# Layer 1 experts: inputs loaded in quarters and turned by VectorE, late tiles in two runs, six of eight output groups combined beside the last tiles

## The chip, the cores and the metric

One core of one Trainium2 chip runs the whole program. The metric is device time in microseconds (us), the median of three runs. A profiled execution is a further run with its own time; all rows of the profile belong to that one. Engines are named as in the profile: PE is TensorE (PEld its weight loads), DVE is VectorE, ACT is ScalarE, POOL is GpSimd, SP is SyncE, which here only issues loads.

## The reference, cut to what matters

The program is a two-layer network on four images of 1024 tokens with 256 channels. Layer 0 (attention, then a mixture of experts) and the first half of layer 1 (selective scans in four directions) are not touched but for one copy. The change is in the second half of layer 1, a mixture of eight experts of which each token uses its best two:

```
logits = xt @ Wr + br
top_p, top_idx = top_k(softmax(logits), 2);  weights = top_p / sum(top_p)
xn = (xt - mean) * rsqrt(var + 1e-5)
for the two experts e of each token:
    xe = xn * ln_g[e] + ln_b[e]                      # 256
    h  = gelu(xe @ W1[e] + b1[e])                    # 1024
    y_e = h @ W2[e] + b2[e]                          # 256
x = x + sum over the two of weights[e] * y_e
```

## The kernel before, in words

**Slots.** Every (token, expert) pair gets a row, a slot, in a table `slots_x` in HBM (258 floats: 256 channels of the normalised token, the number of its result row, its best expert). An expert owns a region of the table; within it pairs stand in order of the images. `norm` (L1680) normalises an image: TensorE makes means (L1689), turns the tokens (L1701) and makes router products (L1703); ScalarE copies the turned tokens to `tok` (L1705), squares them (L1709), copies the products (L1710) and later scales `tok` by a factor that GpSimd raises to a power (L1714 to L1725). `route` (L1597) finds both experts of each token and its slots, on VectorE mostly. `scatter` (L1977) writes the rows, 16 indirect transfers per image, issued by GpSimd (L1981). For images 0 to 2 these are generators whose steps are taken between the operations of the scans (the class from L2005 on, whose order is written out by hand in `turn`, L2134). There the products of the routing lie in the spare of two PSUM buffers that the scans use in turn: TensorE may clear it for the next scan (L2052) only when ScalarE has read the routing out of it, and VectorE's backward scan (L2070) waits for the clearing. For image 3 the routing runs in the expert stage.

**Tiles.** A tile is 256 slots of one expert. `Tiles.fill` (L1574) turns the numbers of slots of each expert into two lists: 17 early tiles (`EARLY`), which images 0 to 2 fill for certain, and late tiles. 36 tiles (`USUAL`) are run; three more stand under a branch that is taken when `extra` says so (L2324). Per tile (class `Tile`, L2219):

- `slots` (L2231): one load of 128 x 2 x 258 floats. `weights` (L2236 to L2246): six loads, of which w1 and w2 are 1 MB each. All are issued by SP, which first reads the expert's or the block's number into a register. The weights have two buffers.
- `inputs` (L2250): TensorE transposes the tile in four 128x128 blocks into PSUM (L2254), VectorE scales it (L2257) and makes the list of result rows `to` (L2260).
- `hidden` (L2263): 16 products of 128x128 by 128x256 (32 matmul rows in the profile; L2269), with a gelu on ScalarE after each pair (L2271); three PSUM buffers of two pieces each.
- `result` (L2273): 16 more products (L2277, again 32 rows), the bias on VectorE (L2280), and two indirect transfers by GpSimd (L2282) that write each result row to its token's place in `results` in HBM. Unused slots go to spare rows at the end of `results`. The framework sees writes to one tensor and makes each wait for the one before.

In this stage the framework's scheduler orders the instructions. It takes two tiles' transposes together, ahead of the first one's matmuls.

**Combination** (L2326 on). When all tiles are done, eight groups of 512 tokens each load both results of each token (1 MB, L2336, by SP), ScalarE multiplies the first by its weight (L2343), VectorE adds the weighted second (L2344), TensorE transposes back (L2347, eight rows), VectorE adds to `x` (L2350), and GpSimd issues two stores (L2351).

Of the kernel before, what the change touches and what calls it, by code (L numbers as in the profile page):

```python
# [11 lines left out]
F32 = mybir.dt.float32  # L12
# [9 lines left out]
P = 128  # L22
# [17 lines left out]
T = 256  # L40
NTILE = 2 * B * L // T + E - 1
# [6 lines left out]
FIRST, SECOND = (2 * (i + 1) * L // T + E - 1 for i in range(2))  # L48
# [14 lines left out]
def metaformer(ctx: ExitStack, tc: tile.TileContext, t: dict, out: bass.AP):  # L63
# [81 lines left out]
    results = dram.tile([2 * B * L + 2 * P, C], F32, tag="results", name="results")  # L145
# [1417 lines left out]
    class Tiles:  # L1563
# [8 lines left out]
        def fill(self, room, tiles, begun):  # L1572

            ends, leap = room([E]), room([E])  # L1574
            past, use, block = room([self.size, E]), room([self.size, E]), room([self.size])
            nc.vector.tensor_tensor_scan(ends, one[:, :E], tiles, 0.0, ALU.mult, ALU.add)
            nc.vector.tensor_tensor(past, ids[:, : self.size].unsqueeze(2).to_broadcast([P, self.size, E]),
                                    ends.unsqueeze(1).to_broadcast([P, self.size, E]), ALU.is_ge)
            nc.vector.tensor_reduce(self.expert, past, AX.X, ALU.add)
            nc.vector.tensor_scalar(self.expert, self.expert, float(E - 1), None, ALU.min)  # L1580

            nc.vector.tensor_tensor(leap, begun[:, 1:], begun[:, :E], ALU.subtract)
            nc.vector.tensor_tensor(leap, leap, tiles, ALU.subtract)
            nc.vector.tensor_scalar(leap, leap, float(BLOCKS), None, ALU.add)
            nc.vector.tensor_tensor(use, past, leap.unsqueeze(1).to_broadcast([P, self.size, E]), ALU.mult)
# [10 lines left out]
    def route(b, tok, slot, space, psum, tag):  # L1596
# [49 lines left out]
        nc.vector.tensor_tensor(place, place, region.unsqueeze(2).to_broadcast([P, E, NT]), ALU.add)  # L1646
        nc.vector.tensor_tensor(count, count, cum[:, :, NT - 1], ALU.add)
# [11 lines left out]
        counts = count.unsqueeze(2).to_broadcast([P, E, BLOCKS])  # L1659
        limits = marks.unsqueeze(1).to_broadcast([P, E, BLOCKS])  # L1660
        if b == B - 2:

            nc.vector.tensor_tensor(more, counts, limits, ALU.is_ge)
            nc.vector.tensor_reduce(tiles, more, AX.X, ALU.add)
            ends = early.fill(room, tiles, done)
            nc.vector.tensor_tensor(left, tiles, ends, ALU.subtract)
            nc.vector.tensor_scalar(left, left, float(EARLY), 0.0, ALU.add, ALU.max)
            nc.vector.tensor_tensor(done[:, :E], left, tiles, ALU.min)
            yield
            yield  # L1670
        else:

            nc.vector.tensor_scalar(count, count, float(T - 1), None, ALU.add)
            nc.vector.tensor_tensor(more, counts, limits, ALU.is_ge)
            nc.vector.tensor_reduce(tiles, more, AX.X, ALU.add)
            nc.vector.tensor_tensor(tiles, tiles, done[:, :E], ALU.subtract)
            ends = late.fill(room, tiles, done)
            nc.vector.tensor_scalar(extra, ends[0:1, E - 1 : E], USUAL - EARLY + 0.5, None, ALU.is_gt)

    def norm(b, tok, pool, psum, tag, raw_tag, d):  # L1680
# [14 lines left out]
        for r in range(NT // 2):  # L1695
# [9 lines left out]
            nc.scalar.copy(tok[:, ts(r, 2), :C], tp)  # L1705
# [270 lines left out]

    def scatter(b):  # L1977

        for n in range(NT):
            for k in range(2):  # L1980
                nc.gpsimd.indirect_dma_start(  # L1981
                    out=slots_x, out_offset=bass.IndirectOffsetOnAxis(ap=slot[:, k, n : n + 1], axis=0),
                    in_=tok[:, n], in_offset=None)
                yield
# [229 lines left out]
    with ExitStack() as st:  # L2214
        of_tiles = st.enter_context(ExitStack())
        pb = of_tiles.enter_context(tc.tile_pool(name="m1_b", bufs=2))
        blocks = slots_x.rearrange("(k a p) c -> k p a c", a=T // P, p=P)

        class Tile:  # L2219
            def __init__(self, tiles, i, tag="xs", bufs=4):  # L2220
                self.tiles, self.i = tiles, i
                self.xs = pb.tile([P, T // P, W], F32, tag=tag, name=tag, bufs=bufs)
# [6 lines left out]
            def slots(self):  # L2229
                block = self.register(1, E * BLOCKS)  # L2230
                nc.sync.dma_start(self.xs, blocks[bass.ds(block, 1)].rearrange("o p a c -> p (o a) c"))  # L2231
# [16 lines left out]
            def inputs(self, ps_t):  # L2248


                tp = ps_t.tile([P, CT, T], F32, tag="tp", name="tp")
                for a in range(T // P):
                    for c in range(CT):
                        nc.tensor.transpose(tp[:, c, ts(a, P)], self.xs[:, a, ts(c, P)], ident)  # L2254
                self.xe = pb.tile([P, CT, T], F32, tag="xe", name="xe")
                for c in range(CT):
                    nc.vector.tensor_scalar(self.xe[:, c], tp[:, c], self.lng[:, c : c + 1],  # L2257
                                            self.lnb[:, c : c + 1], ALU.mult, ALU.add)
                self.to = pb.tile([P, T // P], I32, tag="to", name="to", bufs=NTILE)
                nc.vector.scalar_tensor_tensor(self.to, self.xs[:, :, C + 1], self.tiles.expert[:, self.i : self.i + 1],  # L2260
                                               self.xs[:, :, C], ALU.not_equal, ALU.add)
# [11 lines left out]
            def result(self, ps_y):  # L2273
# [7 lines left out]
                for a in range(T // P):  # L2281
                    nc.gpsimd.indirect_dma_start(  # L2282
                        out=results, out_offset=bass.IndirectOffsetOnAxis(ap=self.to[:, a : a + 1], axis=0),
                        in_=ys[:, a], in_offset=None)

        with ExitStack() as sa:
            pa = sa.enter_context(tc.tile_pool(name="m1_a", bufs=1))
            psa = sa.enter_context(tc.tile_pool(name="m1_psa", bufs=1, space=PSUM))
            ps_t = sa.enter_context(tc.tile_pool(name="m1_ps_t", bufs=2, space=PSUM))
            ps_h = sa.enter_context(tc.tile_pool(name="m1_ps_h", bufs=3, space=PSUM))  # L2290
            ps_y = sa.enter_context(tc.tile_pool(name="m1_ps_y", bufs=1, space=PSUM))

            def run(one_tile):
                one_tile.inputs(ps_t)
# [3 lines left out]
            todo = [Tile(early, i, "xa", EARLY) for i in range(EARLY)]  # L2298
            for i in range(EARLY):
                todo[i].slots()  # L2300
                if i < 2:
                    todo[i].weights()
            b = B - 1
            routing = chain(norm(b, tok, pa, psa, "t", "raw", pa.tile([P, CT, L], F32, tag="nm_d", name="nm_d")),
                            route(b, tok, slot, pa.tile([P, NUMBERS], F32, tag="numbers", name="numbers"), psa, "t"), scatter(b))
            for i in range(EARLY):
                run(todo[i])
                if i + 2 < EARLY:
                    todo[i + 2].weights()
                for _ in range(6):  # L2310
                    next(routing, None)
            assert next(routing, "end") == "end"

            def run_late(which):
                for i in which:
                    one_tile = Tile(late, i)
                    one_tile.slots()
                    one_tile.weights()
# [104 lines left out]
```

## Time and profile before

| | |
|---|---|
| three runs | 3966.72, 3970.53, 3973.8 us (median 3970.53) |
| profiled execution, time | 3952.81 us |
| its span, first to last instruction | 3951.0 us |
| mean clock granted to TensorE | 0.876 |
| busy: PE, DVE, ACT, POOL | 3373.9, 3017.3, 2789.5, 1936.6 us |
| last matmul of the scans' output `y` ends | 3361.8 us |
| first and last expert matmul of layer 1 (start, end) | 3371.0, 3902.9 us |
| loads of w1 and w2 of a tile | 1024 KB each, 5.4 and 5.5 us to landing |
| loads of a tile's inputs (L2231, late tiles) | 258 KB, 4.1 us to landing |

The page of the profile lists busy shares, a picture of the span in 40 slices, the DMA queues, the chain of work that ended last, the costliest groups of instructions and the loads. In a row of a timeline the first number is the start in us, the second the duration, then engine, line, operation, output <- input, shape and count; in brackets is how long the engine had been idle before and what ended that. In a row of the table by windows, the pairs are busy us and instructions (x) of PE, PEld, DVE, ACT and POOL, then the granted clock of TensorE, the DMA engines' share, and GB/s. All rows hold for one profiled execution.

### The profile page before, as it was taken

Reading aid. Unit: us, or ns where it says so; the run is one execution under the profiler, and the core shown is the slowest. Engines: PE = TensorE matmul, PEld = TensorE weight load, DVE = VectorE, ACT = ScalarE, POOL = GpSimd, SP = SyncE. Lnnn points to the kernel's source line nnn. Section 1 sums busy time; section 2 is a strip of 40 time slices with the busy share of each in tenths; the row PEclk is TensorE's granted clock in tenths of the full one; section 3 lists DMA queues with packets and bytes.
Section 4 is the critical chain, followed back from the end, with each engine's and each line's share of the span. In section 5 each row is a group of like instructions: output and inputs, shape, how many; then the busy total and the mean of one; then the engine's idle time right before and its main releaser. Section 6 shows DMA issues by size and latency. Waiting matters only on the chain. (4 is left out here: it accounts for less than half of the span.)

```text
span 3951.0 us, 49637 instructions
## 1 busy us (share of the span) xinstructions
PE 3373.9 (85%) x17330; PEld 1889.9 (48%) x17330; DVE 3017.3 (76%) x5164; ACT 2789.5 (71%) x3738; POOL 1936.6 (49%) x1675
## 2 busy tenths in 40 slices
PE   8378888888788888886697889998998989999996
PEld 5134444534353444543475333443443433788885
DVE  3689899989989898999476899999999999211112
ACT  2889999899989999996244677777767766322222
POOL 0145544675648475575343766556555556121111
PEclk9567887788778777788798999999999999999997
DMA  9400084000000000000384434334334334755555
GB/s 283 121 1 1 1 230 128 1 1 31 12 1 1 1 33 1 1 12 17 97 243 133 142 119 139 118 107 127 120 112 127 125 112 128 223 183 185 189 192 188
DMA packets 241814, 393.71 MB, mean 100 GB/s; under 512 B 31888, under 2 KB 182160, under 8 KB 241424
## 3 DMA queue, kind: packets, MB, share of 16 engines
q1 hardware_dynamic: 218016, 340.54, 28.4%
q0 software_dynamic: 19904, 48.48, 3.8%
q8 instruction: 139, 2.28, 0.2%
q10 hardware_dynamic: 3632, 1.40, 0.1%
q14 instruction: 123, 1.01, 0.1%
HBM read 280.41 MB, written 109.94 MB: 99 GB/s over the span
## 5 line engine op out<-in xcount | busy, mean ns | idle before, releaser
L825 POOL TENSOR_SCALAR dr<-s_n,last 128x1024 bf16<-128x1024 f32 x250 | 715.6, 2880 | 729.5 <-DVE state L853 421.5
L735 ACT ACTIVATE junk_a<-s_n,state 128x1024 int8<-128x1024 f32 x448 | 514.7, 1149 | 23.6 <-DVE state L859 7.3
L2081 POOL TENSOR_TENSOR da_c<-prod,come 128x1024 f32<-128x1024 f32 x128 | 257.5, 2012 | 378.8 <-DVE h L2087 322.7
L739 DVE TENSOR_SCALAR_CACHE_REDUCE junk_v<-s_n,state 128x1024 int8<-128x1024 f32 x320 | 408.6, 1277 | 8.8
L2271 ACT ACTIVATE hid<-hp,b 128x256 f32<-128x256 f32 x288 | 134.1, 474 | 361.1 <-PE hp L2269 361.1
L786 DVE SCALAR_TENSOR_TENSOR w<-s_n,win 128x1024 f32<-128x1024 f32 x256 | 352.0, 1375 | 5.3
L789 DVE MAX8 win<-w 128x8 f32<-128x1024 f32 x256 | 314.5, 1228 | 8.8
L2070 DVE TENSOR_TENSOR_SCAN sum<-da,uu 128x1024 f32<-128x1024 f32 x127 | 289.7, 2281 | 26.5 <-PE sum L2052 19.1
L2092 PE MATMUL sum<-h,ident 128*128 128x512 f32 x512 | 261.4, 635 | 55.6 <-DVE h L2087 52.4
L893 ACT ACTIVATE ex<-sT 128x1024 f32<-128x1024 f32 x256 | 246.9, 1016 | 82.9 <-PE sT L885 82.6
L2046 POOL TENSOR_TENSOR uu<-dx,bb 128x1024 f32<-128x1024 f32 x127 | 303.6, 2390 | 1.7 <-DMA bb<-bc_d 1.6
L735 ACT ACTIVATE junk_a<-s_n,guess 128x1024 int8<-128x1024 f32 x256 | 294.2, 1149 | 7.2
L2063 DVE TENSOR_TENSOR_SCAN h<-da,uu 128x1024 f32<-128x1024 f32 x127 | 288.1, 2269 | 1.0 <-POOL uu L2046 1.0
L2087 DVE TENSOR_TENSOR_SCAN h<-da_c,uu 128x1024 f32<-128x1024 f32 x127 | 288.5, 2272 | 0.0
L2058 PE MATMUL sum<-da_c,ident 128*128 128x512 f32 x512 | 257.2, 626 | 27.3 <-POOL da_c L2081 23.8
L903 PE MATMUL o_ps<-ex,vT 128*32 128x256 f32 x2048 | 236.2, 450 | 50.1 <-ACT ex L893 35.7
L2280 DVE TENSOR_TENSOR ys<-yp,b2e 128x512 f32<-128x512 f32 x36 | 24.9, 691 | 325.7 <-PE yp L2277 325.7
L2030 ACT ACTIVATE da_c<-delta,a_log 128x1024 f32<-128x1024 f32 x128 | 268.0, 2094 | 5.2 <-DMA rows_y<-ys 5.1
L2269 PE MATMUL hp<-xe,w 128*128 128x256 f32 x1152 | 259.0, 383 | 9.4 <-DVE xe L2257 5.9
L2282 POOL DMA_INDIRECT results<-ys,to x72 | 69.3, 963 | 397.0 <-DVE ys L2280 183.6
L769 ACT COPY s_n<-sp 128x1024 f32<-128x1024 f32 x256 | 245.5, 1003 | 23.7 <-PE sp L761 16.0
L2277 PE MATMUL yp<-w2e,hid 128*128 128x256 f32 x1152 | 255.6, 380 | 0.0
(675 smaller groups left out, 7513.9 us busy)
## 6 DMA issues: line engine op xcount, KB each, us to landing
cb<-bc_d SPq DMA_DIRECT2D x128, 512.0 KB, 4.1
bb<-bc_d SPq DMA_DIRECT2D x127, 512.0 KB, 5.0
w<-in_w SPq DMA_DIRECT2D x36, 1024.0 KB, 5.4
w2e<-in_w SPq DMA_DIRECT2D x36, 1024.0 KB, 5.5
slots_x<-zeros SPq DMA_DIRECT2D x1, 33669.0 KB
slots_x<-zeros SPq DMA_DIRECT2D x1, 33282.0 KB
w<-in_w SPq DMA_DIRECT2D x72, 256.0 KB, 3.2
xs<-slots_x SPq DMA_DIRECT2D x36, 261.0 KB, 3.4
```

Of the source, the lines that this page charges most:

```text
L735: nc.scalar.activation(junk, self.row(r), AF.Sign, bias=thr, scale=-1.0, accum_out=u)
L739: nc.vector.tensor_scalar(junk, self.row(r), thr, None, ALU.is_lt, ALU.add, accum_out=u)
L786: nc.vector.scalar_tensor_tensor(w, self.row(r), self.win[:, r, 0:1], self.row(r), ALU.is_gt if r < LAST_DVE else ALU.is_ge, ALU.subtract, ...
L789: nc.vector.max(out=self.win[:, r, 1:], in_=w)
L825: ins = eng.tensor_scalar(dr, self.row(r), self.last[:, r : r + 1], None, ALU.is_lt)
L2030: nc.scalar.activation(grid(self.da_c), cols_flipped(self.prep.delta[:, self.c]), AF.Exp, scale=self.decay)
L2046: nc.gpsimd.tensor_tensor(self.uu[:, 0], self.prep.dx[:, self.c], self.bb, ALU.mult)
L2063: nc.vector.tensor_tensor_scan(rows.rearrange("p r w -> p (r w)"), self.da, self.uu[:, 0], 0.0, ALU.mult, ALU.add)
L2070: nc.vector.tensor_tensor_scan(self.sum[:, ::-1], self.da[:, ::-1], self.uu[:, 0][:, ::-1], 0.0, ALU.mult, ALU.add)
L2087: nc.vector.tensor_tensor_scan(self.hs, self.da_c, self.uu[:, 1], 0.0, ALU.mult, ALU.add)
L2092: nc.tensor.matmul(cols_flipped(self.sum[:, ts(h, HALF)]), ident, grid(self.hs)[:, :, ts(h, half)], start=False, stop=False)
L2269: nc.tensor.matmul(hp[:, f % 2], self.w1[:, c, ts(f, P)], self.xe[:, c], start=(c == 0), stop=(c == CT - 1))
```

## The change

1. **Source order** (`quarters`): when ScalarE copies turned tokens to `tok`, it permutes the channels from (c, q, i) to (q, c, i), with c of 2 halves, q of 4 quarters and i of 32. One copy becomes two.
2. **Quarters**: a tile's inputs are loaded by four loads, one per quarter of the partitions, of 32 x 8 pieces of 64 floats, and a fifth for the two marks of each slot. Tiles are loaded four ahead (`AHEAD`). VectorE transposes 128x512 at once, each 32x32 block by itself, which with the order above gives channels by tokens; then it scales from there. TensorE's transposes and their PSUM buffers go.
3. **Result rows**: `to` is made of three VectorE operations; unused slots get spare rows of their own for each tile, so that no two transfers write the same row, and the framework is told so (`rows_of_their_own`): these writes no longer wait for one another. The same is said of the scatters.
4. **Late tiles in two runs**: first, per expert, all tiles with slots of images 0 to 2; then the rest. After tile 30 (`THIRD` - 1) all results of images 0 to 2 exist.
5. **A written order**: the stage stands in a hand-written order (`usual`): hidden of tile n, inputs of tile n + 1, steps of routing or combination, result of tile n, weights of tile n + 2, slots of tile n + 4, more steps. The 16 scatters of image 3 are issued at once, ahead of tile 13's result.
6. **Combination beside the tiles**: after tile 30 GpSimd issues the loads of the six groups of images 0 to 2; from tile 32 on (`n > THIRD`, 31) each of the two gaps of a tile takes a step: add and store one group, transpose the next, weight the one after; the eight steps end with tile 35. Image 3's two groups come at the end, each loaded in four pieces by SP and ScalarE.

The diff, cut to its core:

```diff
+S = 32
+AHEAD = 4
-FIRST, SECOND = (2 * (i + 1) * L // T + E - 1 for i in range(2))
+FIRST, SECOND, THIRD = (2 * (i + 1) * L // T + E - 1 for i in range(3))
...
         else:
-            nc.vector.tensor_scalar(count, count, float(T - 1), None, ALU.add)
-            nc.vector.tensor_tensor(more, counts, limits, ALU.is_ge)
-            nc.vector.tensor_reduce(tiles, more, AX.X, ALU.add)
-            nc.vector.tensor_tensor(tiles, tiles, done[:, :E], ALU.subtract)
-            ends = late.fill(room, tiles, done)
+            both_, begun = room([2 * E]), room([2 * E + 1])
+            nc.vector.tensor_copy(begun[:, :E], done[:, :E])
+            nc.vector.memset(begun[:, 2 * E :], 0.0)
+            nc.vector.tensor_scalar(tiles, before, float(T - 1), None, ALU.add)
+            whole_tiles(begun[:, E : 2 * E], tiles)
+            nc.vector.tensor_tensor(both_[:, :E], begun[:, E : 2 * E], done[:, :E], ALU.subtract)
+            yield
+            nc.vector.tensor_scalar(tiles, count, float(T - 1), None, ALU.add)
+            whole_tiles(left, tiles)
+            nc.vector.tensor_tensor(both_[:, E:], left, begun[:, E : 2 * E], ALU.subtract)
+            yield
+            ends = late.fill(room, both_, begun, 2 * E)
...
-            nc.scalar.copy(tok[:, ts(r, 2), :C], tp)
+            for c in range(CT):
+                nc.scalar.copy(quarters(tok[:, ts(r, 2), :C])[:, :, c],
+                               tp[:, :, ts(c, P)].rearrange("p n (q i) -> p n q i", i=S))
...
+    def rows_of_their_own(ins, group):
+        tc.declare_no_dep(ins, group=group, reason="rows of their own")
+        tc.add_to_no_dep_group(group, ins)
...
-                nc.sync.dma_start(self.xs, blocks[bass.ds(block, 1)].rearrange("o p a c -> p (o a) c"))
+                self.xs = pb.tile([P, T // S, width], F32, tag="xs", name="xs", bufs=AHEAD + 1)
+                for q in range(P // S):
+                    nc.sync.dma_start(self.xs[ts(q, S)], pieces[q][bass.ds(block, 1)].rearrange("o t i c -> t (o i) c"))
+                self.meta = pb.tile([P, T // P, W - C], F32, tag="meta", name="meta", bufs=AHEAD + 1)
+                nc.sync.dma_start(self.meta, marked[bass.ds(block, 1)].rearrange("o p a c -> p (o a) c"))
...
-                tp = ps_t.tile([P, CT, T], F32, tag="tp", name="tp")
-                for a in range(T // P):
-                    for c in range(CT):
-                        nc.tensor.transpose(tp[:, c, ts(a, P)], self.xs[:, a, ts(c, P)], ident)
+                xt = pb.tile([P, T // S, CT, S], F32, tag="xt", name="xt")
+                nc.vector.transpose(xt.rearrange("p i c t -> p (i c t)"), self.xs.rearrange("p i c -> p (i c)"))
...
+            def load(self):
+                self.y = pc.tile([P, 4, 2 * C], F32, tag="y", name="y")
+                if self.b < B - 1:
+                    ins = nc.gpsimd.dma_start(self.y, by_pairs[self.g]).ins
+                    rows_of_their_own(ins, "last_results")
+                    nc.gpsimd.memset(apart, 0.0)
+                else:
+                    for i in range(4):
+                        (nc.scalar if i % 2 else nc.sync).dma_start(self.y[:, i], by_pairs[self.g][:, i])
...
+        def combining():
+            for g in range(len(some) + 2):
+                if g > 1:
+                    some[g - 2].store()
+                if 0 < g <= len(some):
+                    some[g - 1].turn()
+                if g < len(some):
+                    some[g].combine()
+                yield
...
+            def between(n):
+                for _ in range(2):
+                    next(routing, None)
+                if n > THIRD:
+                    next(combined, None)
+
+            todo[0].inputs()
+            for n in range(USUAL):
+                todo[n].hidden(ps_h)
+                if n + 1 < USUAL:
+                    todo[n + 1].inputs()
+                between(n)
+                if n == EARLY - AHEAD:
+                    assert next(routing, "end") == "end"
+                    for _ in scatter(b):
+                        nc.gpsimd.memset(apart, 0.0)
+                todo[n].result(ps_y)
+                if n == THIRD - 1:
+                    for group in some:
+                        group.load()
+                if n + 2 < USUAL:
+                    todo[n + 2].weights()
+                if n + AHEAD < USUAL:
+                    todo[n + AHEAD].slots()
+                between(n)
...
+        for group in groups[len(some) :]:
+            group.load()
+        for group in groups[len(some) :]:
+            group.combine()
+            group.turn()
+            group.store()
```

`turn` makes eight transposes of 128x128 into two PSUM buffers; `store` adds them to `x` and issues two stores; `combine` is ScalarE's product and VectorE's sum, four of each.

## The prediction

> **What bounds the kernel now.** I read the cores view first (one core, span 3951.0 us, mean clock 0.876), then the table by windows over the stretch that the change rewrites. Columns: busy time of each engine, clock granted to TensorE, share of the DMA engines, GB/s.
>
> ```profile
> 3350.00:3400.00 50.00, 47.05 (x209) 34.33 (x208) 15.38 (x37) 13.15 (x36) 4.83 (x4) 1.00 0.76 243
> 3800.00:3850.00 50.00, 49.28 (x235) 42.32 (x234) 7.05 (x15) 12.58 (x27) 6.73 (x7) 1.00 0.58 192
> 3900.00:3951.00 51.00, 18.47 (x78) 13.24 (x76) 23.73 (x49) 13.65 (x32) 10.65 (x18) 0.55 0.67 253
> ```
>
> In the expert stage TensorE is busy 49.3 of 50 us; VectorE has 7, the DMA engines 0.58. The last 51 us are another stage: TensorE is nearly idle there. TensorE's own timeline shows the period of a pair of tiles:
>
> ```profile
> 3786.07 1.04 PE L2254 MATMUL tp<-ident,xs 128*128 128x128 f32 x8
> 3787.47 7.19 PE L2269 MATMUL hp<-xe,w 128*128 128x256 f32 x32 [0.36 <-DVE xe L2257]
> 3794.50 7.07 PE L2277 MATMUL yp<-w2e,hid 128*128 128x256 f32 x32
> 3801.41 7.09 PE L2269 MATMUL hp<-xe,w 128*128 128x256 f32 x32
> 3808.33 7.07 PE L2277 MATMUL yp<-w2e,hid 128*128 128x256 f32 x32
> 3815.24 1.04 PE L2254 MATMUL tp<-ident,xs 128*128 128x128 f32 x8
> ```
>
> A pair takes 29.16 us (3787.47 to 3816.63), of which the four blocks of matmuls take 27.66 and the turning of the inputs, with the 0.36 us wait behind it, 1.50. Then the end of the whole timeline:
>
> ```profile
> 3902.93 0.69 DVE L2280 TENSOR_TENSOR ys<-yp,b2e 128x512 f32<-128x512 f32 x1 [13.14 <-PE yp L2277]
> 3906.56 0.96 POOL L2282 DMA_INDIRECT results<-ys,to  x1 [1.71 <-DMA results<-ys,to]
> 3915.93 1.71 ACT L2343 ACTIVATE y<-y,wts 128x256 f32<-128x256 f32 x4 [19.44 <-DMA y<-results]
> 3943.61 1.29 DVE L2350 TENSOR_TENSOR x<-op,x 128x512 f32<-128x512 f32 x2 [0.68 <-PE op L2347]
> ```
>
> From TensorE's last expert matmul, T = 3902.9, it is 13 us to the first product of the combination, then eight groups at 3.55 us each, then 6.1 us from the last addition's end (3944.9) to the end of the span: 48.1 us. So the program's end is 3371.0 (first expert matmul) + 531.9 + 48.1.
>
> **The change part by part**, against the profiled execution (span 3951.0, time 3952.81; the median of the three runs is 3970.53, 17.7 above it; I carry the difference over unchanged).
>
> (a) *TensorE no longer turns inputs.* 18 pairs at 1.50: **-27.0 us**, all on the path. VectorE takes it: one transpose of 128x512 and two scalings per tile. No row shows its transpose. The nearest row is the 128x512 addition, 0.69 us; the Trainium skill (VectorE: DVE Perf Modes, The three transpose paths) gives 311 ns for a 128x128 block in bf16, an estimate of 1.24 us for four. That page also advises TensorE for a 128x128 transpose when PSUM will do as destination. By that rule the change picks the wrong engine; by the windows row TensorE is the bound and VectorE has 43 of 50 us free. A tile asks VectorE for at most 1.24 + 1.07 (scalings) + 0.69 + three small operations of 0.2 = 3.6 us in 13.83, and the built order puts a tile's inputs one whole tile ahead. I take 0 on the path; only the first tile pays it. Gaining is excluded too.
>
> (b) *Inputs come in quarters.* A tile's 256 packets of 1032 B become 1024 of 256 B and 256 of 8 B. The hardware queue's row from 3500 to 3850 us (50218 packets, 58.38 MB, 52.3% of sixteen engines) gives 58 ns a packet. Today's transfers take 0.58 x 14.58 = 8.5 us of each tile. At no cost per packet but bytes, nothing changes; at 58 ns for each of 1280 packets, 4.7 us come and 0.9 go: 12.3 of 13.83 us, still under the period. The Trainium skill (DMA: Bandwidth & Descriptors, Specifications) sets 512 B as the least for full rate; charging 256 B as 512 B is an estimate of +0.26 MB, about 1 us at the 304 GB/s that the whole queue's row gives while busy. All three fit; 0 on the path, since inputs are asked for four tiles ahead.
>
> (c) *Start of the stage.* Before, tile 0's inputs are the first load; the first expert matmul waited for the last small weight, landed at 3370.2. Now w1, four small ones and w2 go first, then the quarters; in the built program the fourth quarter must await the completion of the load eight places earlier, the scale, which lands about 3369.2. It then lands behind w2 and three quarters, at about 3373.3; transpose and scaling 1.5 us: first matmul at about 3375, **+4** (+2 to +8). Between 3362 and 3371 TensorE did 6.5 us of image 3's routing: eight rows at 0.43, 22 raw at 0.12, four transposes at 0.11. The written-out order puts all of it after tile 0: **+6.5**. And TensorE now idles 12 us. The cost of idling is in these rows:
>
> ```profile
> 3404.00:3408.00 4.00, 2.49 (x12) 1.81 (x10) 1.76 (x9) 0.41 (x1) 3.58 (x6) 1.00 0.82 282
> 3408.00:3412.00 4.00, 2.05 (x6) 1.55 (x7) 1.50 (x8) 2.98 (x8) 2.01 (x3) 0.82 0.09 33
> 3412.00:3416.00 4.00, 4.00 (x15) 3.41 (x15) 0.00 (x0) 3.29 (x7) 0.00 (x0) 0.75 0.02 4
> ```
>
> After a 3.46 us stall the clock is 0.82 and 0.75 for 8 us, some 1.7 us lost: **+1.7** here.
>
> (d) *Routing in a written order.* That 3.46 us stall was ScalarE's eight scalings of the tokens waiting for GpSimd's powers. In the new order GpSimd reaches the second power only after tile 3's two scatters: end of tile 3's matmuls + 0.9 + 2.2 (two issues) + 2.9 (the chain 3406.08 to 3409.0) = 6.0; the scalings take 3.6; tile 4's activations stand behind them, from 9.7. TensorE fills three PSUM buffers (5.2 us) and waits until 10.6: 5.4 + 1.7 of clock = 7.1 against today's 5.2, **+1.9**.
>
> (e) *The early scatters lose their waits on one another* (157 us of GpSimd waiting on its own results): off the path, 0, except in the tail.
>
> (f) *Six of eight groups are combined beside tiles 32 to 35.* Their 48 transposes run at full clock, 1.04 us per eight (in the tail, at 0.50, 1.94): **+6.2** on TensorE. The 6 MB of loads are issued by GpSimd when all results of tiles 0 to 30 have landed: end of tile 30 + 0.9 + 1.1 + 5.3 = 7.3. For the software queue's pace, its page row (19904 packets of 2436 B in 3.8% of 16 x 3951 us) gives 121 ns a packet, 3.2 us per MB alone, 6.5 if it shares evenly with the weights. With issue and landing I take 9.5 us for the first group: there at 16.8. It is first asked for by ScalarE behind tile 32's activations, at 20.7, and by TensorE ahead of tile 33, at 27.7. The second, at 20 to 23.3, is asked for right behind the first; who waits for it are tile 33's activations, which three PSUM buffers let come as late as 32.9. **0** for the wait (0 to 8).
>
> (g) *The tail has two groups.* Scatters issue together: at T + 1.0 and 2.05, landed and seen 2.96 later: T + 5.0 instead of 6.6. Eight quarter-MB loads from two queues; the page's 256 KB loads take 3.2 us, and 2 MB at the tail's 401 GB/s 5.2: all there at about T + 12.2. Last product and sum 1.0, transposes 0.5, additions 1.3: T + 15. Then 6.1 as before, and 0.4 for the branch: T + 21.5. **-26.6** (-21 to -29).
>
> (h) *Tokens written in source order.* One copy of 128x512 becomes two of half size, 0.59 against twice 0.38, in 12 turns of the scans. There ScalarE's small row is followed by TensorE's clearing of a sum and by VectorE, which waits 0.68 us in each of these turns:
>
> ```profile
> 2530.62 0.59 ACT L1705 COPY tok<-sum 128x512 f32<-128x512 f32 x1 [0.89 <-PE sum L1703]
> 2531.99 0.16 ACT L1710 COPY lg<-sum 128x16 f32<-128x16 f32 x1
> 2532.24 0.60 PE L2052 MATMUL sum<-nought 128*128 128x512 bf16 x2
> 2532.93 2.30 DVE L2070 TENSOR_TENSOR_SCAN sum<-da,uu 128x1024 f32<-128x1024 f32 x1 [0.68 <-issue]
> ```
>
> 12 x 0.18 = **+2.2** (0 to 4).
>
> (i) *Two runs of late tiles* leave 36 tiles; the longer tables are some 20 more VectorE operations of 0.2 to 0.4 us under tile matmuls: 0. The 16 scatters of image 3 hold SP's queue (loads of tile 16's weights stand behind tile 17's inputs) until about 24 us after tile 12; those weights are due at 41: 0, or up to 5 if each scatter waits out its landing.
>
> Sum: -27.0 + 4 + 6.5 + 1.7 + 1.9 + 6.2 - 26.6 + 2.2 = **-31.1 us**. Span about 3920, profiled time 3922, median **3939**.
>
> **The rivals.**
> 1. *As summed*, 3930 to 3949: 0.53. A measurement of this kernel can tell about 0.2%, 8 us, from no change.
> 2. *More is hidden*: the first tile is ready like today's, no cold clock, ScalarE's wait in (d) as short as today's: -31.1 - 4 - 1.7 - 1.9, about 3931 or below. For it: the first loads meet emptier DMA engines than today (1.0 share from 3376 to 3400, when seventeen tiles' inputs are fetched at once). Against: the written order, which nothing can fill. 0.12.
> 3. *The loads of (f) and the weights slow each other*: TensorE waits once per tile in the last four for weights or a group, 4 us each: -15, 3955. For it: the 1.0 share wherever many loads meet. 0.17 (0.155 faster, 0.015 same).
> 4. *Slower: the software queue can't keep pace.* ScalarE takes the sixth group before tile 35's activations, wanted by about 65 after tile 30 (four tiles of 13.83, five turnings, 5.2 of buffers). The groups arrive at 16.8 + 5p; beyond p = 9.6 us per MB each further us costs five, beyond 15.8 (66 GB/s) the gain is gone. At 18: +11, 3981. Against: 3.2 to 6.5. 0.11.
> 5. *It doesn't do what it says*: small packets cost more than the mean packet, the DMA engines become the bound and the tile period stays near 14.5: a loss of 0.7 x 36 = 25 of the 31: -6, 3965. For it: the upper end of (b) is a share of 0.89. 0.07 (0.065 same, 0.005 faster).
>
> Faster 0.53 + 0.12 + 0.155 + 0.005 = 0.81, same 0.08, slower 0.11. The range 3928 to 3959 takes in cases 1 and 2 and most of 3, and leaves 4 and 5 out.
>
> **What would show it.** Right: no input transposes on TensorE, tile period 13.8, first expert matmul near 3377 (scans 2 us longer), one 5 us gap in tile 4's hidden blocks, no gap before the `op` transposes of tiles 32 to 35, 21 to 22 us from the last expert matmul to the end. Wrong: TensorE waiting for `xe` or weights in mid-stage (b); gaps after tile 31 with ScalarE on `y` (f); a tail over 25 us (g); scan turns unchanged or longer by far more than 0.2 us (h).

## The result: slower, and where the profile after puts it

The changed kernel takes 4065.98 us (median of four runs, 4056.39 to 4071.52); the kernel before took 3968.62 us in runs beside it (3958.74 to 3973.8). The ratio is 1.0246, with a 95% interval of 1.0217 to 1.0275: slower by 2.5%. The forecast was 3939 us, and the sign was wrong. The profiled execution of the changed kernel has a span of 4069.8 us, 118.8 us more than that of before.

First the same table by windows as before the prediction (busy time of each engine, clock granted to TensorE, share of the DMA engines, GB/s), for the changed kernel at the start, in the middle and at the end of the expert stage:

```profile
3350.00:3400.00 50.00, 39.48 (x88) 18.58 (x88) 27.70 (x29) 14.04 (x13) 16.05 (x14) 0.83 0.49 141
3850.00:3900.00 50.00, 43.08 (x187) 34.10 (x186) 7.22 (x21) 11.38 (x24) 6.64 (x12) 1.00 0.53 163
4018.00:4069.00 51.00, 29.88 (x140) 23.29 (x140) 14.30 (x28) 11.26 (x25) 10.06 (x18) 0.80 0.28 104
```

In the middle TensorE was busy for 49.3 of 50 us; now for 43.1, at full clock, and no other column has grown to speak of: VectorE has the 7 us it had, the DMA share has fallen from 0.58 to 0.53. So TensorE waits for something that is itself not busy. TensorE's timeline shows for what:

```profile
3844.27 7.07 PE L2312 MATMUL yp<-w2e,hid 128*128 128x256 f32 x32
3851.17 1.03 PE L2304 MATMUL hp<-xe,w 128*128 128x256 f32 x4
3852.82 1.99 PE L2304 MATMUL hp<-xe,w 128*128 128x256 f32 x8 [0.61 <-ACT hid L2306]
3855.37 1.99 PE L2304 MATMUL hp<-xe,w 128*128 128x256 f32 x8 [0.56 <-ACT hid L2306]
3857.93 1.99 PE L2304 MATMUL hp<-xe,w 128*128 128x256 f32 x8 [0.56 <-ACT hid L2306]
3860.49 1.13 PE L2304 MATMUL hp<-xe,w 128*128 128x256 f32 x4 [0.56 <-ACT hid L2306]
3861.46 2.75 PE L2312 MATMUL yp<-w2e,hid 128*128 128x256 f32 x12
```

The turning of the inputs is gone from TensorE, as announced. But the hidden block, one row of 32 matmuls in 7.19 us before, now falls into five pieces with four waits for ScalarE's gelu. From one `yp` block to the next it is 17.19 us: 10.29 for the hidden block (3851.17 to 3861.46) and 6.90 for the other. Before, a tile took 14.58; the prediction had 13.83. The table of waits of TensorE in the expert stage (total, times, longest) confirms that this is one wait, repeated; first before, then after:

```profile
PE hp L2269 <- DVE xe L2257: 5.9, 16, 0.5
PE hp L2269 <- ACT hid L2271: 3.5, 1, 3.5
```

```profile
PE hp L2304 <- ACT hid L2306: 96.1, 144, 9.2
PE hp L2304 <- DVE xe L2288: 6.8, 1, 6.8
```

144 is four for each of 36 tiles. The groups of the page say it once more: ScalarE's gelu has not become slower, 474 ns each as before; of the 102.9 us that TensorE stands idle ahead of its hidden matmuls, 96.1 end with a gelu.

```profile
L2306 ACT ACTIVATE hid<-hp,b 128x256 f32<-128x256 f32 x288 | 136.6, 474 | 456.6 <-PE hp L2304 439.7
L2304 PE MATMUL hp<-xe,w 128*128 128x256 f32 x1152 | 306.6, 406 | 102.9 <-ACT hid L2306 96.1
```

The end of the timeline is as announced: the last `yp` matmul ends at 4045.7, and the last addition to the image starts 16.5 us behind it instead of 40.7 us.

```profile
4045.72 0.69 DVE L2315 TENSOR_TENSOR ys<-yp,b2e 128x512 f32<-128x512 f32 x1 [14.28 <-PE yp L2312]
4048.01 0.99 POOL L2317 DMA_INDIRECT results<-ys,to  x1 [0.19 <-issue]
4054.54 0.97 ACT L2349 ACTIVATE y<-y,wts 128x256 f32<-128x256 f32 x2 [16.13 <-DMA y<-results]
4062.24 1.29 DVE L2362 TENSOR_TENSOR x<-op,x 128x512 f32<-128x512 f32 x2 [0.60 <-PE op L2357]
```

Cut at four marks (the first and the last forward scan of the scans, the first and the end of the last expert matmul), the two executions compare so:

| us | before | after | difference |
|---|---|---|---|
| up to the first scan | 2175.6 | 2190.4 | +14.8 |
| first to last scan (start to start) | 1169.9 | 1173.4 | +3.5 |
| last scan to first expert matmul | 25.5 | 22.1 | -3.4 |
| expert stage | 531.9 | 659.8 | +127.9 |
| tail | 48.1 | 24.1 | -24.0 |
| span | 3951.0 | 4069.8 | +118.8 |

The first row has no edit in its work that could carry it: it is code that the change leaves alone, and in the ten kernels profiled here the first scan starts anywhere from 2175.6 to 2191.1. That is scatter from one execution to another, and it is why the experiments are read by the rows below it as well as by the time.

**Where the order comes from.** In the code the two loops are nearly alike: for each f (one of the eight blocks of 128 hidden channels) two matmuls into half f % 2 of a PSUM tile, then a gelu that reads that half. What differs is who orders them. In the kernel before, the scheduler took the first halves of two PSUM tiles ahead of their second halves; the hand-written order keeps them as they stand. These are TensorE's sixteen matmuls of one tile's hidden block in the built order (the profile counts each as two), each named by its PSUM buffer, A to D in turn; a star marks one that waits for ScalarE:

```
before: A B A B C A* A B* B C D* D C* C D* D
after:  A A A* A B B B* B C C C* C D D D* D
```

Half of the tiles of before have this order; the others begin A A B B and end as this one does. Both kernels have the wait: the first matmul into the second half of a buffer waits for the gelu of the first half. (The first D* of before waits for the buffer that A leaves.) Before, two or three other matmuls stood between a first half and its star, 0.43 us each, so that the gelu was over when TensorE came there. After, nothing stands between. The Trainium skill (PSUM — Partial Sum Buffer, PSUM bank collisions raise a hardware error) gives the reason for such a wait: TensorE may not write into a bank while another engine reads that bank in the same partitions, at whatever address, so accesses are to be guarded by bank. A buffer of 128x512 in f32 is one bank by that page; its two halves can't be in use by two engines at once. No run here shows a collision, and a kernel with the wait merely struck out was not tried.

### The profile page after: what moved, and what is told of

It is laid out like the page before. It is cut to its first block, busy times and chain, and to the rows that moved or that the text cites. A ratio compares the mean times of both kernels' runs of the same rounds, so it can differ in the third digit from the quotient of the medians.

```text
span 4069.8 us, 49999 instructions
## 1 busy us (share of the span) xinstructions
PE 3408.9 (84%) x17186; PEld 1880.0 (46%) x17186; DVE 3044.3 (75%) x5282; ACT 2793.2 (69%) x3754; POOL 1954.4 (48%) x1776
## 3 DMA queue, kind: packets, MB, share of 16 engines
q1 hardware_dynamic: 253536, 333.21, 27.0%
## 5 line engine op out<-in xcount | busy, mean ns | idle before, releaser
L737 ACT ACTIVATE junk_a<-s_n,state 128x1024 int8<-128x1024 f32 x448 | 514.6, 1149 | 23.9 <-DVE state L861 8.3
L2304 PE MATMUL hp<-xe,w 128*128 128x256 f32 x1152 | 306.6, 406 | 102.9 <-ACT hid L2306 96.1
L2304 PEld LDWEIGHTS hp<-xe,w 128*128 128x128 f32 x1152 | 214.6, 197 | 189.2 <-ACT hid L2306 156.4
L2087 PE MATMUL sum<-da_c,ident 128*128 128x512 f32 x512 | 257.1, 626 | 25.9 <-POOL da_c L2110 22.3
```

Source lines behind the costliest of these rows:

```text
L737: nc.scalar.activation(junk, self.row(r), AF.Sign, bias=thr, scale=-1.0, accum_out=u)
L2087: nc.tensor.matmul(self.sum[:, ts(h, HALF)], ident if eye is None else eye, view[:, ts(h, HW // NHALF), :], start=False, stop=last)
L2304: nc.tensor.matmul(hp[:, f % 2], self.w1[:, c, ts(f, P)], self.xe[:, c], start=(c == 0), stop=(c == CT - 1))
```

## The experiments

The theory: the wait between the two halves of a PSUM tile, which the hand-written order leaves uncovered, costs 3.36 us a tile, 121 us in all, and the rest of the prediction holds. The rivals: the longer period is due to the inputs in quarters, or to VectorE's turning. All times below are medians beside runs of the kernel before on the same chip: 3959.36 us (11 runs) for the first four kernels, 3961.77 us (15 runs) for the other four.

### e1: both halves filled, then both read

```diff
-                for f in range(NF):
-                    if f % 2 == 0:
-                        hp = ps_h.tile([P, 2, T], F32, tag="hp", name="hp")
-                    for c in range(CT):
-                        nc.tensor.matmul(hp[:, f % 2], self.w1[:, c, ts(f, P)], self.xe[:, c],
+                for f0 in range(0, NF, 2):
+                    hp = ps_h.tile([P, 2, T], F32, tag="hp", name="hp")
+                    for f in (f0, f0 + 1):
+                        for c in range(CT):
+                            nc.tensor.matmul(hp[:, f % 2], self.w1[:, c, ts(f, P)], self.xe[:, c],
...
-                    nc.scalar.activation(self.hid[:, f], hp[:, f % 2], AF.Gelu, bias=self.b1[:, f : f + 1])
+                    for f in (f0, f0 + 1):
+                        nc.scalar.activation(self.hid[:, f], hp[:, f % 2], AF.Gelu, bias=self.b1[:, f : f + 1])
```

> The changed kernel with one thing altered: both halves of a hidden PSUM tile are filled before ScalarE reads either (matmuls f, f+1, then two gelus). Theory (TensorE's first matmul into the second half waits for ScalarE's gelu of the first half, about 0.86 us four times a tile): the wait goes, a tile takes 13.8 us instead of 17.2, 36 x 3.36 = 121 us: 3945 us (3938 to 3955). Rival (the quartered loads or VectorE's turning set the longer period): the period stays near 17.2 and the time at 4060 to 4070.

Measured: 3930.35 us, ratio 0.9924 (0.9905 to 0.9943): 0.76% below before, with an interval clear of 1, and below the theory's range. TensorE's timeline of e1 is whole again:

```profile
3747.37 7.07 PE L2304 MATMUL hp<-xe,w 128*128 128x256 f32 x32
3754.28 7.07 PE L2313 MATMUL yp<-w2e,hid 128*128 128x256 f32 x32
3761.18 7.07 PE L2304 MATMUL hp<-xe,w 128*128 128x256 f32 x32
```

and of the 144 waits one is left in its table of waits for the stage:

```profile
PE hp L2304 <- DVE xe L2288: 6.9, 1, 6.9
PE hp L2304 <- ACT hid L2307: 5.3, 1, 5.3
```

A tile takes 13.81 us (3747.37 to 3761.18). The stage is 521.5 us, 138 less than after the change. The instructions, the loads and VectorE's work are the same as in the changed kernel; only the order of matmuls and gelus within a pair of f differs. The rivals fall. The drop in time is 136 us (128 by the two ratios), more than the theory's 121; the section on the prediction shows where the rest is.

### e2: each f in a bank of its own

```diff
                 for f in range(NF):
-                    if f % 2 == 0:
-                        hp = ps_h.tile([P, 2, T], F32, tag="hp", name="hp")
+                    hp = ps_h.tile([P, T], F32, tag="hp", name="hp")
```

(`hp[:, f % 2]` becomes `hp` in the two lines that use it.)

> The changed kernel, its order kept (two matmuls, a gelu, two matmuls, a gelu), but each f has a PSUM tile of its own, three in rotation, instead of half of one. Theory (it is the sharing of a tile by two halves that makes the wait, not the alternation): no wait, since three tiles give 2.6 us of runway against about 1.3 us from a matmul's end to its tile's release: 3945 us (3938 to 3957). Rival A (alternation of matmuls and gelus is what costs): 4060 to 4070. Rival B (loads or VectorE): 4060 to 4070 too, and told from A by e1.

Measured: 3933.22 us, ratio 0.9943 (0.9927 to 0.9958), again below the theory's range; the stage 525.8 us, a tile 13.81 us. Here the order still alternates, two matmuls and a gelu, and the waits are gone all the same. So it is not the alternation but the sharing of one PSUM tile, which is one bank: in the built program of e2 the three buffers lie in three banks. Whether two tiles within one bank would wait as well was not tried. Half of each bank lies idle in e2, and there is one stall more than in e1 (two waits for gelus, 9.2 us together, against one of 5.3); a likely reason, not tested, is that three banks with one f each hold less work for TensorE than three with two.

### e3: the scheduler orders the changed kernel

```diff
-        with tc.manual_schedule():
-            usual()
+        usual()
```

> The changed kernel without its hand-written order: the scheduler orders the same instructions, and in the built order takes the first halves of two PSUM tiles before the second halves, as in the kernel before. Theory: the 121 us of waits go here too; what the scheduler does with the loads, the routing and the combination may cost or gain some 15 us: 3945 us (3925 to 3965). Rival (loads or VectorE): 4060 to 4070.

Measured: 3975.91 us, ratio 1.0046 (1.0031 to 1.006): 90 us less than the changed kernel (79 by the two ratios), and yet 0.46% above before and outside what was expected. The 144 waits are gone, as the theory has it, but another has come; its timeline, TensorE and VectorE:

```profile
3757.41 0.69 DVE L2315 TENSOR_TENSOR ys<-yp,b2e 128x512 f32<-128x512 f32 x1 [12.75 <-PE yp L2312]
3758.02 0.73 DVE L2288 TENSOR_SCALAR xe<-xt,lng,lnb 128x256 f32<-128x256 f32 x2
3758.48 7.19 PE L2304 MATMUL hp<-xe,w 128*128 128x256 f32 x32 [1.10 <-DVE xe L2288]
3758.78 0.71 DVE L2285 STREAM_TRANSPOSE xt<-xs 128x512 f32<-128x512 f32 x1
```

The scheduler puts the scaling of the next tile's inputs on VectorE behind the addition that ends this tile. VectorE had been idle for 12.75 us, and TensorE waits for it 29 times in the 36 tiles, 34.4 us in all and 1.10 us in the steady ones: there the period is 15.2 us. So the hand-written order did earn something. It puts a tile's inputs ahead of the previous tile's result, which takes this wait, and the 1.39 us between 15.2 and 13.81, off the path; in the same stroke it uncovered the wait of 3.4 us.

### e4: the same wait in the kernel before

```diff
                 one_tile.inputs(ps_t)
-                one_tile.hidden(ps_h)
-                one_tile.result(ps_y)
+                with tc.manual_schedule():
+                    one_tile.hidden(ps_h)
+                    one_tile.result(ps_y)
```

> The kernel before, with only its hidden and result matmuls put in a hand-written order as the changed kernel has them (two matmuls, a gelu). In the built order the first halves are followed at once by the second halves, save where four transposes or the next tile's first matmuls stand between. Theory: two to four waits of 0.86 us a tile: 36 x (1.7 to 3.4) = +62 to +121, so 4031 to 4090 us, likeliest 4060, with the old inputs and loads. Rival (loads in quarters or VectorE's turning): nothing of these is in this kernel, 3965 to 3980.

Measured: 4004.8 us, ratio 1.0113 (1.0094 to 1.0133): 45 us slower than before, below the lower end of the theory's range, far above the rival's. TensorE's timeline:

```profile
3752.38 1.89 PE L2269 MATMUL hp<-xe,w 128*128 128x256 f32 x8
3754.10 0.60 PE L2254 MATMUL tp<-ident,xs 128*128 128x128 f32 x4
3754.83 2.00 PE L2269 MATMUL hp<-xe,w 128*128 128x256 f32 x8
3757.39 3.72 PE L2269 MATMUL hp<-xe,w 128*128 128x256 f32 x16 [0.56 <-ACT hid L2271]
3760.95 7.07 PE L2277 MATMUL yp<-w2e,hid 128*128 128x256 f32 x32
```

I had counted two to four uncovered waits a tile; there is one. The other three are covered by transposes, by a neighbouring tile's first matmuls or by its whole result block, which the scheduler puts in between. One uncovered wait shows the same 0.56 us of idling as after the change, and a tile takes 15.47 us (3752.38 to the next hidden block at 3767.85, in the same view) instead of 14.58: 0.89 more for one wait, 32 us in all. The stage is 42.4 us longer; of the other 10 us only a part is known, the longest wait for a gelu, now 9.6 us instead of 3.5. Without quarters and without VectorE's turning, the order alone brings the wait.

### e5: e1 with TensorE turning the inputs

Tokens in plain order, one load a tile, and in the inputs:

```diff
-                xt = pb.tile([P, T // S, CT, S], F32, tag="xt", name="xt")
-                nc.vector.transpose(xt.rearrange("p i c t -> p (i c t)"), self.xs.rearrange("p i c -> p (i c)"))
+                tp = psa.tile([P, HALF], F32, tag="t", name="tp").rearrange("p (c t) -> p c t", c=CT)
+                for half in range(T // P):
+                    for c in range(CT):
+                        nc.tensor.transpose(tp[:, c, ts(half, P)], self.xs[:, half, ts(c, P)], ident)
```

> The kernel of e1 (3930 us, stage 521.5 us from the first expert matmul to the last) with its inputs as in the kernel before: tokens in plain order, one load a tile, four transposes a tile on TensorE, emitted between a tile's hidden and result matmuls. Theory, step (a) of the prediction: TensorE has 36 x 0.6 to 0.75 us more to do, +22 to +27 in the stage, so 3954 us (3948 to 3960), and a period near 14.5 us. Rival (the turning hid in waits, or VectorE's turning costs as much elsewhere): 3930 to 3936.

Measured: 3943.17 us, ratio 0.9959 (0.9944 to 0.9974); 13 us slower than e1, less than expected and below the range. Its stage is 542.1 us, 20.6 more. TensorE's timeline:

```profile
3760.22 7.07 PE L2301 MATMUL hp<-xe,w 128*128 128x256 f32 x32
3767.12 0.60 PE L2283 MATMUL tp<-ident,xs 128*128 128x128 f32 x4
3767.56 7.07 PE L2310 MATMUL yp<-w2e,hid 128*128 128x256 f32 x32
3774.47 7.07 PE L2301 MATMUL hp<-xe,w 128*128 128x256 f32 x32
```

A tile takes 14.25 us, 0.44 more than in e1: 15.9 us for 36 tiles. (The rest of the 20.6 contains 4.1 us of waiting ahead of the combination's transposes, for which the profile names no releaser.) So VectorE's turning is worth 0.44 us a tile. The other 0.33 us of the 0.77 between 14.58 and 13.81 goes with the place in the order: with the transposes a block ahead, TensorE no longer waits for the scaling behind them. (The table of waits of before shows 5.9 us of this, 0.16 a tile; the rest is not itemised.)

### e6: e1 with all eight groups at the end

```diff
-        some = groups[: (B - 1) * NHALF]
+        some = []
...
-                    ins = nc.gpsimd.dma_start(self.y, by_pairs[self.g]).ins
-                    rows_of_their_own(ins, "last_results")
-                    nc.gpsimd.memset(apart, 0.0)
+                    nc.sync.dma_start(self.y, by_pairs[self.g])
```

> The kernel of e1 with all eight groups combined at the end, from loads on the synchronous engine's queue (the last two groups' as in e1). Theory, steps (f) and (g): the stage loses the 48 transposes (-6.2), the tail grows from 24.3 to about the 48.1 us of before (+23.8): 3948 us (3942 to 3955). Rival (the six loads and combinations beside tiles 32 to 35 disturb the stage by much more than the 6.2 us): the stage gains over 12 us and the time stays below 3942.

Measured: 3944.57 us, ratio 0.9961 (0.9947 to 0.9976). The stage is 516.4 us (-5.1), the tail 46.4 (+22.1): a net 17.0, and 14.2 by the times. Theory holds, the rival falls: the combination beside tiles 32 to 35 costs the stage what its transposes take and little else. The row by windows for the tail of e6 looks like that of before, with TensorE at 0.50 of its clock:

```profile
3900.00:3942.00 42.00, 15.87 (x64) 10.78 (x64) 23.15 (x48) 13.67 (x32) 8.75 (x16) 0.50 0.81 303
```

### e7 and e8: the two stalls that are left

e7 is e1 with both of GpSimd's powers in one step, for image 3 only:

```diff
         nc.gpsimd.tensor_tensor(s1, ve, minus_half, ALU.pow)
-        yield
-        yield
+        if b < B - 1:
+            yield
+            yield
         nc.gpsimd.tensor_tensor(ve, s1, s1, ALU.mult)
```

> The kernel of e1 with GpSimd's second power of image 3's norm computed right behind the first (two yields fewer), so that ScalarE's eight scalings come behind tile 3's gelus instead of ahead of tile 4's. Theory, step (d): the 5.28 us stall of TensorE in tile 4 and about 1.7 us at a lower clock behind it go: the stage 514.5 us, the time 3923 (3918 to 3928, execution scatter apart). Rival (the wait moves to another step of the routing, or to the early scatters): the stage stays at 519 to 523.

Measured: 3922.25 us, ratio 0.9895 (0.9874 to 0.9917). ScalarE's scalings now stand behind tile 3's gelus, while TensorE does tile 3's `yp` block, and tile 4's hidden block is whole:

```profile
3441.59 7.07 PE L2314 MATMUL yp<-w2e,hid 128*128 128x256 f32 x32
...
3442.52 3.29 ACT L1751 ACTIVATE tok<-tok,nm_s 128x256 f32<-128x256 f32 x8
3448.50 7.07 PE L2305 MATMUL hp<-xe,w 128*128 128x256 f32 x32
```

The stage is 513.5 us, 8.0 less than in e1, against 7.0 expected. The intervals of the two ratios overlap (0.9905 to 0.9943 in e1), so it is the trace that shows the gain and not the times.

e8 is e7 with earlier scatters and tile 0's inputs ahead of its weights (`spare` is a tile of one element):

```diff
             next(sending, None)
+            if k >= len(order) - 4:
+                nc.gpsimd.memset(spare, 0.0)
+                next(sending, None)
...
+                if n == 0:
+                    todo[n].slots()
                 if n < 2:
                     todo[n].weights()
-                todo[n].slots()
+                if n > 0:
+                    todo[n].slots()
```

> The kernel of e7, with two scatters instead of one in each of the last turns of the scans, and tile 0's inputs asked for before its weights. Theory: tile 0's quarters wait for the last scatters to land (issued 10 us behind the last scan's start); now they are asked for some 6 us earlier, and the first expert matmul comes 5 us after TensorE's last matmul of the scans or less, instead of 6.9 us, with less time at a low clock: 3916 us (3910 to 3922). Rival (the loads wait for the scans' memory, or the first weights then land later by as much): no change, 3923, or the scatters slow the last scans by 1 us a turn: 3926.

Measured: 3915.95 us, ratio 0.9888 (0.987 to 0.9907), the lowest of all. From the timeline:

```profile
3366.32 1.22 DVE L2137 SCALAR_TENSOR_TENSOR x<-y,x 128x1024 f32<-128x1024 f32 x1 [2.21 <-PE y L2132]
3367.47 0.70 DVE L2290 STREAM_TRANSPOSE xt<-xs 128x512 f32<-128x512 f32 x1
3369.58 0.74 DVE L2293 TENSOR_SCALAR xe<-xt,lng,lnb 128x256 f32<-128x256 f32 x2 [1.41 <-DMA lnb<-in_ln_b]
3370.30 9.68 PE L2309 MATMUL hp<-xe,w 128*128 128x256 f32 x32 [4.02 <-issue]
```

The turning no longer waits for the quarters; the scaling now waits for a small weight instead, the wait that the kernel before had here too. From the last scan to the first expert matmul it is 19.4 us instead of 22.6, half of the 7 us expected, and the slow first block is as long as it was (9.68 us against 9.65 in e1); the scans took 1.1 us longer than in e7, the stage 1.4; the scans of like kernels differ by as much here. By the times e7 and e8 can't be told apart (their intervals overlap); the trace shows the 3.2 us. That the time falls on the 3916 forecast is luck. The two edits were not tried apart.

The stretches of all eight and of the two first kernels, from their profiled executions:

| us | scans | to first expert matmul | stage | tail | a tile |
|---|---|---|---|---|---|
| before | 1169.9 | 25.5 | 531.9 | 48.1 | 14.58 |
| after | 1173.4 | 22.1 | 659.8 | 24.1 | 17.19 |
| e1 pairs | 1170.0 | 22.3 | 521.5 | 24.3 | 13.81 |
| e2 own banks | 1170.1 | 22.3 | 525.8 | 23.9 | 13.81 |
| e3 scheduler | 1171.8 | 33.4 | 564.3 | 22.7 | 15.20 |
| e4 before, ordered | 1170.4 | 25.8 | 574.3 | 48.3 | 15.47 |
| e5 TensorE turns | 1171.6 | 22.2 | 542.1 | 24.5 | 14.25 |
| e6 all at the end | 1171.8 | 22.4 | 516.4 | 46.4 | 13.81 |
| e7 powers | 1172.1 | 22.6 | 513.5 | 23.9 | 13.81 |
| e8 start | 1173.2 | 19.4 | 514.9 | 24.0 | 13.81 |

## Why the prediction was wrong

**The step that failed** is the one taken for granted: "the four blocks of matmuls take 27.66", read off the kernel before and carried into (a), under an order that the change rewrites. Step (a) costed what left TensorE and never asked what the new order does to what stays: those four blocks, two tiles' worth, took 34.38 us (twice 17.19). The built order of the changed kernel was at hand, and it shows the wait on ScalarE at the first matmul of every second half. In (d), "TensorE fills three PSUM buffers (5.2 us)" ahead of ScalarE is the same error: in the written order it can fill half of one. To count buffers was not enough; what counts is how many matmuls stand between a gelu and the next writer of its bank. None of the five rivals was about this. The fourth and fifth looked at queues and DMA engines; in the middle of the stage these have room (a share of 0.53 after the change, 0.63 from 3700 to 3750 us in e1), and TensorE is busy for all 50 us from 3850 to 3900 in e1, where the six groups are loaded.

**How much it was.** Eight matmuls without a wait take 1.73 us (6.91 / 4); with it the rows follow at 2.56 us (3852.82 to 3855.37 and on). That is 0.83 a wait, of which 0.56 is shown as idle; four in a tile, and the measured period is 3.38 above e1's: 36 x 3.38 = 122 us. The stage lost 138 against e1. The other 16 us are where the same order meets a slow clock or a busy ScalarE: tile 0's hidden block (3385.95 to 3403.98, 18.0 us, against 9.5 in e1, so 5 beyond the steady 3.4), the stall of (d) at 9.23 instead of 5.28 us (3.4 beyond), and tile 5, whose second matmuls wait 3.45 us behind a step of the routing on ScalarE and its table load, and then run at half clock (18.5 us from 3498.73 to 3517.21, against 10.3: 8.2).

With this one thing mended, in e1, the sum comes out. Forecast: 3939 of 3970.53, a ratio of 0.9921; e1: 0.9924. That it is so close is in part luck: by the table's rows e1 has -10.4 us in the stage for -10.7 forecast, but -3.2 for +4 at its start, -23.8 for -26.6 in the tail and +0.1 for +2.2 in the scans, 37.3 us less in all instead of 31.1 (one profiled execution of each kernel). By its steps:

(a) -27.0. The period in e1 fell by 0.77 us, 36 x 0.77 = 27.7: size right, in the order of e1. e5 shows that only 15.9 of it is VectorE's turning; the rest goes with the earlier place of the inputs. After the change as it stood, the period rose by 2.61.

(b) 0 on the path: right. The hardware queue moved 253536 packets instead of 218016, with a share of 27.0% against 28.4% of a shorter span; no wait for inputs shows in mid-stage. The smaller packets are not free, but far from 58 ns each: between 3500 and 3850 us the trace after has 18 ns on average for one of 256 B, the trace before 47 ns for one of 1032 B, so a tile's inputs take 1.2 us of the sixteen engines instead of 0.8.

(c) Wrong in sign for the wait: +4 was expected, and the first expert matmul comes 3.4 us sooner behind the last scan. The times of that step follow from a first load at about 3362, as before. But there tile 0's inputs stood first in SP's queue and waited 21.6 us for the last scatter, so that the first load went out 16.5 us behind the start of the last scan, with the weights behind it; now the weights stand first and go out at 9.9 us, and the quarters, which still wait for the scatter, at 15.9. The 6.5 of routing moved into the stage as expected (its first row, of 1.88 us, stands behind tile 0's hidden block in e1). The clock cost 2.6 us in e1 (the first 32 matmuls in 9.65 us instead of 7.07) for 1.7 expected. e8, with the scatters earlier and tile 0's quarters ahead of the weights, takes 3.2 us more off the start.

(d) 5.4 + 1.7 expected, 5.28 and a slower row behind it in e1: right there, 9.23 after the change. e7 took it away and gained 8.0.

(e), (i) 0: no wait of TensorE points to them.

(f) +6.2 and no wait: e6 gives 5.1 back. Right.

(g) T + 21.5 expected; 24.1 after, 24.3 in e1. The loads were issued at T + 5.0 as worked out; they were all there a little later than 12.2 (the last product that waits for one starts at T + 13.9), and the last products and sums of two groups follow one another instead of overlapping: mis-sized by 2.6 to 2.8 us.

(h) +2.2: not settled. The scans took 1169.9 and 1170.4 us with one copy, 1170.0 to 1173.4 with two, but 1171.6 in e5, which has one again. An effect of 2 us can't be told from this scatter.

## What to carry to other kernels

When a change moves work from a scheduler to an order written by hand, read the built order of the work that stays, not only of what is moved: for every buffer that two engines share, count what the producer can do between its last write ahead of the consumer and its own next write to the same bank. Fill the whole bank, then read it, or give each consumer step a bank of its own; both took the wait away here. And a period measured under one order is no constant of the matmuls; it belongs to the order.

## What the runs showed of the hardware beside this

How long TensorE stayed at half clock at the start of the stage differed between the kernels. These rows by windows are of the changed kernel, from the first expert matmul on (the column ahead of the last two is the granted clock):

```profile
3386.00:3390.00 4.00, 2.02 (x5) 1.12 (x5) 0.43 (x4) 1.76 (x2) 0.00 (x0) 0.50 1.05 358
3390.00:3394.00 4.00, 3.75 (x8) 2.50 (x8) 0.00 (x0) 0.68 (x2) 0.00 (x0) 0.50 0.83 167
3394.00:3398.00 4.00, 3.68 (x8) 2.52 (x8) 1.81 (x6) 0.74 (x2) 0.00 (x0) 0.50 0.47 89
3398.00:3402.00 4.00, 3.44 (x9) 2.52 (x8) 0.00 (x0) 0.95 (x2) 0.00 (x0) 0.50 0.18 30
3402.00:3406.00 4.00, 3.44 (x12) 1.90 (x11) 0.10 (x1) 0.95 (x2) 0.00 (x0) 0.87 0.12 28
```

and these are of e1, from its first expert matmul on:

```profile
3383.40:3387.40 4.00, 4.00 (x10) 3.19 (x11) 0.41 (x4) 0.14 (x1) 0.00 (x0) 0.50 1.06 361
3387.40:3391.40 4.00, 4.00 (x18) 3.46 (x17) 0.00 (x0) 2.90 (x6) 0.00 (x0) 0.87 0.83 176
```

The changed kernel stayed at half clock for 16 us, the last 12 of them with 0.56 us of idling in every 4.35 us; e1, without the idling, for about 5. Yet in mid-stage the same 0.56 us, now in every 2.56, left the clock at 1.00. The Trainium skill (TensorE: Matmul & The Clock Gate, Part 1: The HAM clock gate) has the clock rise after about 3.4 us of sustained work. e1 took about 5; in the changed kernel's tile 0, TensorE busy for 3.44 to 3.75 us of each 4 was not enough. But the idling alone does not decide. In tile 4 of the same kernel, behind its long stall, one block at half clock and one wait of 0.56 us were followed by full clock:

```profile
3481.51 3.67 PE L2304 MATMUL hp<-xe,w 128*128 128x256 f32 x8 [9.23 <-ACT hid L2306]
3485.74 1.99 PE L2304 MATMUL hp<-xe,w 128*128 128x256 f32 x8 [0.56 <-ACT hid L2306]
```

In tile 5 it took three such blocks again. What makes the difference no run here shows.

VectorE's transpose of 128x512 in f32 took 0.70 us (the row in e8), where the prediction estimated 1.24 from a figure for bf16.
